# Where the second products of an expert and of a feed-forward stand in a stream that gives way to attention

## The chip, the cores and the metric

The kernel runs on one core of one Trainium2 chip. TensorE (PE in the profile) does the matrix products, with its weight loads (PEld) shown apart; VectorE (DVE), ScalarE (ACT) and GpSimd (POOL) do the element-wise work, and SyncE (SP) issues most transfers. Each engine works through its own instructions in a fixed order, which is settled when the program is built, and waits on semaphores for the others. The metric is the device time of one execution in microseconds: 1697.75 us is the median of three runs of the kernel before (1693.24 to 1705.93).

## The reference

The input is 2048 tokens of 128 float32 features. Two layers follow, each with a layernorm and a residual ahead of each half:

- layer 0, first half: a state-space mixer (8 heads, 16 states) with a gate;
- layer 0, second half: a block of its own, `x1 = x + attention(layernorm(x))`, and then `x1 + moe(layernorm(x1))`. The attention is causal, with 16 heads of 8 features over all 2048 tokens. The mixture has 8 experts of width 512, of which the two best of each token count; each expert is `gelu(n @ fc1.T + b1) @ fc2.T + b2`, scaled by the token's gate;
- layer 1, first half: a selective scan (256 channels, 16 states);
- layer 1, second half: a feed-forward, `h = silu(x w1) * (x w2)`, `h = gelu(h h1)`, `h = gelu(h h2)`, `h w3`, of width 512.

Everything is float32. All eight experts are computed for every token, and the gate of an expert that was not chosen is zero.

## The kernel before

**Chunks and stages.** The tokens are cut into four chunks of 512 (`NC`, `C`). Features lie on the 128 partitions, tokens along the free side, so most products are 128 by 128 times 128 by 512. The stages of a chunk are Python generators: `ssd`, `experts`, `scan`, `feed`, and for the attention `prepare`, `shift`, `weighted`, `conclude`. Each `yield` hands over with a number, the cost that the author gives to the piece just emitted.

**Attention beside the rest.** `with_attention` runs the generator of the stages, and after each piece of cost w it lets the attention go on until it has emitted pieces worth `w * RATE`. So a `yield` is a place where the stream of stages gives way, and its number says for how much attention. The attention goes job by job, a chunk of queries and a group of four heads: `shift` finds the maximum of the scores (products L304 into `ps_m`, mask L313, maximum on DVE L314), and `weighted` recomputes scores transposed (L354 into `ps_e`), adds the shift (L360), masks the diagonal (L362), takes the exponential on ACT (L364) and sums values (L341 into `ps_o`). `weighted` of one job and `shift` of the next are emitted in step. Each of `ps_m` and `ps_e` is one buffer of two banks, so a pair of score products waits until DVE, or ACT, has read the pair before. One pair of L354, its L360 pair and its exponential are called a step of attention here.

**An expert.** `experts` goes through the eight experts in pairs. For each pair it emits eight first products (L797, into the two buffers of `ps_a`), each followed by a gelu on ACT (L798). Then it yields 7.4, and the second products follow (L803): four of them sum into the single buffer of `ps_c`, one for each quarter of the hidden features, with a yield of 0.9 after each but the last. DVE adds the bias and multiplies by the gate (L807), POOL adds to the sum of the experts (L809), and a yield of 0.8 follows.

**Gelu and exponential take turns.** ACT has to load another table (a record of its own in the trace) between a gelu and an exponential. `in_turn` puts an order between the two kinds, so that the eight gelus of a pair stand together on ACT, and an exponential of the attention that is emitted after them waits behind them.

**A feed-forward.** `feed` has two inner layers (L954): for each of four output quarters f, four products k sum into a buffer of `ps_a`, with a yield of 0.9 after each but the last and 0.8 after the quarter. The gelus (L960) of two quarters are emitted together, behind every odd quarter. The third layer (L966) follows.

**What settles the order.** The emitted order gives priorities alone. A scheduler places the instructions on each engine, by its own estimate of when each is ready, so an instruction that is emitted later can stand earlier where the one ahead of it would wait. The result is the order of the built program.

**The tail.** The last chunk has no attention left beside it. It is cut into two halves of 256 tokens, and `abreast` alternates between `experts`, `scan` and `feed` of the halves and the `feed` of chunk 2, always taking the thread that is furthest behind by the sum of its yields. There the numbers of the yields decide how finely the threads alternate.

Of the kernel before, what the change touches and what calls it, by code (L numbers as in the profile page):

```python
# [24 lines left out]
NB = C // P  # L25
# [17 lines left out]
NF = FF // P  # L43
# [29 lines left out]
def two_layers(ctx: ExitStack, tc: tile.TileContext, a: dict, out: bass.AP):  # L73
# [27 lines left out]
    def col(name, i=0, n=P, w=1):  # L101
        at = COL[name][0] + i
        return cols[:n, at : at + w]
# [143 lines left out]
    def after_stage(*names):  # L247
        while not written.issuperset(names):
            yield None
# [471 lines left out]
    def part(c):  # L721

        c, lo, n = c if isinstance(c, tuple) else (c, 0, NB)
        return c, slice(lo, lo + n), n, n * P
# [3 lines left out]
    def turn(kind):  # L728
        used[kind] = used.get(kind, 1) ^ 1
        return used[kind]  # L730
# [6 lines left out]
    def experts(c, z):  # L737
        c, bs, NB, C = part(c)
        yield from after_stage(("attention", c))
        x = xc[c][:, bs]  # L740
        nx = z.blocks("xn", NB)
        layernorm(nx, xa[c][:, bs])
        pt = transposed(nx, z.bank)
        nT = z.line("nT", (P, C))
        nc.vector.tensor_scalar(nT, pt, col("ln2_w"), col("ln2_b"), ALU.mult, ALU.add)
        yield 1.0 * NB / 4

        pl = z.bank([P, NB, NE])
        for b in range(NB):
            nc.tensor.matmul(pl[:, b, :], nT[:, b * P : (b + 1) * P], w_eg, start=True, stop=True)  # L750
        lg = small_tile("lg", [P, NB, NE])
        nc.vector.tensor_copy(lg, pl)

        full = [P, NB, NE, NE]
        other = lg.unsqueeze(2).to_broadcast(full)
        own = lg.unsqueeze(3).to_broadcast(full)
        gt = small_tile("gt", full)
        eq = small_tile("eq", full)
        nc.vector.tensor_tensor(gt, other, own, ALU.is_gt)
        nc.vector.tensor_tensor(eq, other, own, ALU.is_equal)  # L760
        nc.vector.tensor_tensor(eq, eq, before8.unsqueeze(1).to_broadcast(full), ALU.mult)
        nc.vector.tensor_tensor(gt, gt, eq, ALU.add)
        rank = small_tile("rank", [P, NB, NE])
        nc.vector.tensor_reduce(rank, gt, AX.X, ALU.add)
        top = small_tile("etop", [P, NB])
        nc.vector.tensor_reduce(top, lg, AX.X, ALU.max)
        ge = small_tile("ge", [P, NB, NE])
        nc.vector.tensor_tensor(ge, lg, top.unsqueeze(2).to_broadcast([P, NB, NE]), ALU.subtract)
        nc.scalar.activation(ge, ge, AF.Exp)
        nc.vector.scalar_tensor_tensor(ge, rank, 1.5, ge, ALU.is_lt, ALU.mult)  # L770
        nc.vector.tensor_reduce(top, ge, AX.X, ALU.add)
        nc.vector.reciprocal(top, top)
        nc.vector.tensor_tensor(ge, ge, top.unsqueeze(2).to_broadcast([P, NB, NE]), ALU.mult)
        pgt = z.bank([NE, C])
        for b in range(NB):
            nc.tensor.transpose(pgt[:, b * P : (b + 1) * P], ge[:, b], ident)
        gT = z.line("gT", (NE, C))
        nc.vector.tensor_copy(gT, pgt)
        gates = scratch_g[turn("gates")][:, 0:C]
        nc.sync.dma_start(gates, gT)  # L780
        yield 1.5 * NB / 4

        acc = z.line("acc", (P, C))

        for e0 in range(0, NE, 2):
            of = []
            for e in (e0, e0 + 1):
                we = z.wide()
                nc.sync.dma_start(we[:, 0], a["fc1"][e])
                nc.sync.dma_start(we[:, 1].rearrange("p (k d) -> p k d", k=NF), a["fc2"][e].rearrange("(k p) d -> p k d", p=P))  # L790
                gb = z.line("gb", (P, C))
                nc.sync.dma_start(gb, gates[e].partition_broadcast(P))
                hs = [z.four("h", C) for _ in range(2)]
                of.append((we, gb, hs))
                for f in range(NF):
                    ph = z.bank([P, C])
                    nc.tensor.matmul(ph, we[:, 0, f * P : (f + 1) * P], nT, start=True, stop=True)  # L797
                    in_turn("gelu", nc.scalar.activation(hs[f // 2][:, f % 2, :], ph, AF.Gelu, bias=col("fc1_b", e * NF + f)))  # L798
            yield 7.4 * NB / 4
            for e, (we, gb, hs) in zip((e0, e0 + 1), of):  # L800
                py = z.sum([P, C])
                for f in range(NF):
                    nc.tensor.matmul(py, we[:, 1, f * P : (f + 1) * P], hs[f // 2][:, f % 2, :], start=f == 0, stop=f == NF - 1)  # L803
                    if f < NF - 1:
                        yield 0.9 * NB / 4
                dst = acc if e == 0 else z.line("ye", (P, C))
                nc.vector.scalar_tensor_tensor(dst, py, col("fc2_b", e), gb, ALU.add, ALU.mult)  # L807
                if e:
                    nc.gpsimd.tensor_tensor(acc, acc, dst, ALU.add)  # L809
                yield 0.8 * NB / 4  # L810
        pt = z.bank([P, NB, D])
        for b in range(NB):
            nc.tensor.transpose(pt[:, b, :], acc[:, b * P : (b + 1) * P], ident)
        nc.vector.tensor_tensor(x, x, pt, ALU.add)
        yield 1.0 * NB / 4
# [102 lines left out]
    def feed(c, z):  # L918
        c, bs, NB, C = part(c)
        x = xc[c][:, bs]  # L920
        nx = z.blocks("xn", NB)
        layernorm(nx, x)
        pt = transposed(nx, z.bank)
        nT = z.line("nT", (P, C))
        nc.vector.tensor_copy(nT, pt)
        w12 = z.wide()
        nc.sync.dma_start(w12[:, 0], a["w1"])
        nc.sync.dma_start(w12[:, 1], a["w2"])
        w3 = z.pool.tile([P, NF, D], F32, tag="w3", name="w3", bufs=1) if z.width < FF else z.blocks("w3")
        nc.sync.dma_start(w3, a["w3"].rearrange("(k p) o -> p k o", p=P))  # L930
        h = [z.four("h", C) for _ in range(2)]
        for f in range(NF):
            p1 = z.bank([P, C])
            nc.tensor.matmul(p1, w12[:, 0, f * P : (f + 1) * P], nT, start=True, stop=True)
            p2 = z.bank([P, C])
            nc.tensor.matmul(p2, w12[:, 1, f * P : (f + 1) * P], nT, start=True, stop=True)
            s = z.line("s", (P, C))
            in_turn("exp", nc.scalar.activation(s, p1, AF.Tanh, scale=half_s[:, f : f + 1]))
            nc.vector.scalar_tensor_tensor(s, s, 1.0, p1, ALU.add, ALU.mult)
            nc.vector.scalar_tensor_tensor(h[f // 2][:, f % 2, :], p2, both_s[:, f : f + 1], s, ALU.mult, ALU.mult)  # L940
            if f % 2:
                yield 3.5 * NB / 4
        for name, scale in (("h1", "h1_s"), ("h2", "h2_s")):
            w = []
            for i in range(2):
                w.append(z.wide())
                nc.sync.dma_start(w[i], a[name][2 * i * P : 2 * (i + 1) * P].rearrange("(k p) o -> p k o", p=P))
            g = [z.four("g", C) for _ in range(2)]
            phs = []
            for f in range(NF):  # L950
                ph = z.bank([P, C])
                phs.append(ph)
                for k in range(NF):
                    nc.tensor.matmul(  # L954
                        ph, w[k // 2][:, k % 2, f * P : (f + 1) * P], h[k // 2][:, k % 2, :], start=k == 0, stop=k == NF - 1
                    )
                    if k < NF - 1:
                        yield 0.9 * NB / 4
                for i in range(f - 1, f + 1) if f % 2 else ():
                    in_turn("gelu", nc.scalar.activation(g[i // 2][:, i % 2, :], phs[i], AF.Gelu, scale=col(scale, i)))  # L960
                yield 0.8 * NB / 4
            h = g
        po = z.sum([P, NB, D])
        for b in range(NB):
            for k in range(NF):
                nc.tensor.matmul(  # L966
                    po[:, b, :], h[k // 2][:, k % 2, b * P : (b + 1) * P], w3[:, k, :], start=k == 0, stop=k == NF - 1
                )
        res = z.blocks("xn", NB)
        nc.vector.tensor_tensor(res, po, row("w3_s").unsqueeze(1).to_broadcast([P, NB, D]), ALU.mult)  # L970
        nc.gpsimd.tensor_tensor(res, res, x, ALU.add)  # L971
        nc.sync.dma_start(x_out[c][:, bs], res)
        yield 3.6 * NB / 4
# [162 lines left out]
```

## Time and profile before

| what | value |
| --- | --- |
| median of three runs | 1697.75 us |
| the profiled execution, its own time | 1707.93 us |
| its span in the profile | 1706.2 us |
| PE busy | 1488.6 us, 87% |
| DVE busy | 983.1 us, 58% |
| ACT busy | 670.4 us, 39% |
| POOL busy | 265.1 us, 16% |
| mean granted TensorE clock | 0.847 |
| table loads on ACT, each | 1.283 us |

The profiled execution is 10.2 us longer than the median. The span is divided in time as follows: up to about 430 us the first layer's mixer, with the first attention jobs beside it from 160 us on; from 450 us to about 1450 us experts, scans and feed-forwards of chunks 0 to 2 with the attention; from there the tail. The twelve batches of eight gelus with attention beside them lie between 451 and 1209 us, four for each of the chunks 0, 1 and 2. A row of the view by windows gives, for a stretch of time, the busy time of PE, PEld, DVE, ACT and POOL with the number of their instructions, then the granted clock, the busy share of the DMA engines and GB/s. In the view of instructions in order of time, a row gives the start, the length, the engine, the line, the operation, and in brackets the idle time of the engine before it. A float32 product of 128 by 128 times 128 by 512 shows as two PE records.

### The profile page before, as it was taken

What the parts mean: (1) busy time and instruction counts of PE and PEld (TensorE: products, weight loads), DVE (VectorE), ACT (ScalarE), POOL (GpSimd) and SP (SyncE); (2) the same over time, 40 slices, a digit from 0 to 9 for tenths busy, and PEclk for the clock granted to TensorE, in tenths of its full rate; (3) what the DMA queues carried; (4) which work ended last, traced back from release to release, by engine and by line L of the source; (5) the groups of instructions that cost most, each with busy time, mean ns of one, the idle gap of its engine ahead of it and who ended that gap; (6) DMA issues with size and microseconds to landing.
All of it is one profiled execution on the core that took longest, in us unless ns stands there. A gap on an engine that the chain in (4) does not pass through costs nothing. (4 is left out here: it accounts for less than half of the span.)

```text
span 1706.2 us, 17298 instructions
## 1 busy us (share of the span) xinstructions
PE 1488.6 (87%) x6550; PEld 679.7 (40%) x6550; DVE 983.1 (58%) x1670; ACT 670.4 (39%) x864; POOL 265.1 (16%) x332
## 2 busy tenths in 40 slices
PE   6998999999999889887979868999888796889787
PEld 3554445454332333232333333433322232555355
DVE  4566546666444464658486878443568741337672
ACT  2212222332434334534425525445436463346351
POOL 3332011211000010122020122000001121112100
PEclk9898878898999787968779878887988876799798
DMA  2000000000211001246121535120103731334131
GB/s 87 1 1 1 1 0 1 1 1 1 79 38 37 25 25 33 76 103 142 35 52 32 123 74 112 38 62 29 40 24 68 151 80 32 114 100 129 40 91 52
DMA packets 73874, 90.93 MB, mean 53 GB/s; under 512 B 5672, under 2 KB 40696, under 8 KB 73792
## 3 DMA queue, kind: packets, MB, share of 16 engines
q1 hardware_dynamic: 61120, 65.18, 12.7%
q0 software_dynamic: 12240, 23.60, 8.2%
q8 instruction: 51, 0.84, 0.2%
q10 hardware_dynamic: 432, 1.06, 0.2%
q14 instruction: 31, 0.25, 0.1%
HBM read 64.98 MB, written 1.25 MB: 39 GB/s over the span
## 5 line engine op out<-in xcount | busy, mean ns | idle before, releaser
L314 DVE TENSOR_REDUCE top<-ps_m 128x2 f32<-128x1024 f32 (+3 forms) x320 | 339.5, 1061 | 267.9 <-PE ps_m L313 130.4
L364 ACT ACTIVATE probs<-ps_e 128x1024 f32<-128x1024 f32 (+3 forms) x320 | 286.6, 895 | 495.1 <-PE ps_e L360 268.0
L304 PE MATMUL ps_m<-kR,qR 32*128 32x512 f32 (+3 forms) x640 | 181.5, 519 | 57.7 <-DVE top L314 49.4
L354 PE MATMUL ps_e<-qR,kR 32*128 32x512 f32 (+3 forms) x640 | 174.0, 519 | 41.4 <-ACT probs L364 40.7
L884 DVE TENSOR_TENSOR_SCAN db<-da,hlast,db 128x512 f32<-128x512 f32 (+1 forms) x160 | 166.2, 1081 | 44.9 <-ACT da L880 44.2
L341 PE MATMUL ps_o<-probs,vv 128*9 128x512 f32 (+3 forms) x1152 | 175.0, 602 | 0.9 <-ACT probs L364 0.9
L304 PEld LDWEIGHTS ps_m<-kR,qR 32*128 32x128 f32 x640 | 74.1, 205 | 219.0 <-DVE top L314 127.1
L354 PEld LDWEIGHTS ps_e<-qR,kR 32*128 32x128 f32 x640 | 69.1, 204 | 200.5 <-ACT probs L364 132.6
L803 PE MATMUL ps_c<-h,wide 128*128 128x512 f32 (+1 forms) x320 | 142.5, 556 | 4.3 <-DVE ye L807 4.2
L360 PE MATMUL ps_e<-sh,onesR 32*128 32x512 f32 (+3 forms) x640 | 145.3, 430 | 1.1 <-DVE sh L326 1.1
L797 PE MATMUL ps_a<-nT,wide 128*128 128x512 f32 x192 | 107.5, 691 | 1.7 <-ACT h L798 1.6
L809 POOL TENSOR_TENSOR acc<-acc,ye 128x512 f32<-128x512 f32 (+1 forms) x35 | 41.1, 1174 | 395.8 <-DVE ye L807 360.4
L888 POOL COPY hlast<-db 128x2 f32<-128x2 f32 x64 | 26.7, 417 | 463.9 <-DVE db L884 456.5
L882 DVE TENSOR_TENSOR db<-du,bb 128x1024 f32<-128x1024 f32 (+1 forms) x80 | 79.9, 1016 | 20.2 <-DMA bb<-scratch_b 7.3
L798 ACT ACTIVATE h<-ps_a,cols 128x512 f32<-128x512 f32 x96 | 64.9, 687 | 54.4 <-PE ps_a L797 54.3
L880 ACT ACTIVATE da<-dl 128x1024 f32<-128x1024 f32 (+1 forms) x80 | 67.3, 880 | 29.7 <-DVE db L884 18.9
L803 PEld LDWEIGHTS ps_c<-h,wide 128*128 128x128 f32 x320 | 57.0, 198 | 52.4 <-issue 38.1
L360 PEld LDWEIGHTS ps_e<-sh,onesR 32*128 32x128 f32 x640 | 74.8, 219 | 6.2 <-issue 4.1
L954 PE MATMUL ps_a<-g,wide 128*128 128x512 f32 x96 | 60.4, 745 | 2.7 <-DVE sz L905 1.8
L797 PEld LDWEIGHTS ps_a<-nT,wide 128*128 128x128 f32 x192 | 35.6, 214 | 58.1 <-ACT h L798 39.7
L954 PE MATMUL ps_a<-h,wide 128*128 128x512 f32 x96 | 55.1, 678 | 0.0
L891 PE MATMUL ps_o<-db,ident 128*128 128x512 f32 x64 | 35.7, 640 | 7.7 <-DVE db L884 7.6
(376 smaller groups left out, 2072.2 us busy)
## 6 DMA issues: line engine op xcount, KB each, us to landing
wide<-in_fc SPq DMA_DIRECT2D x80, 256.0 KB, 3.2
bb<-scratch_b SPq DMA_DIRECT2D x48, 256.0 KB, 3.3
db<-db POOLq DMA_DIRECT2D x24, 512.0 KB, 5.5
u<-db POOLq DMA_DIRECT2D x21, 512.0 KB, 5.6
wide<-in_h SPq DMA_DIRECT2D x20, 512.0 KB, 3.9
gb<-scratch_g SPq DMA_DIRECT2D x24, 256.0 KB, 4.1
bb<-scratch_b SPq DMA_DIRECT2D x32, 128.0 KB, 3.0
wide<-in_w SPq DMA_DIRECT2D x10, 256.0 KB, 2.8
```

Source lines behind the costliest of these rows:

```text
L304: nc.tensor.matmul(pss[:, j, 0:n], qR[hr, w - P : w], kR[hr, g, kc * C : kc * C + n], start=True, stop=not diag,)
L314: nc.vector.tensor_reduce(top[:, i : i + 2, kc], pss[:, :, 0:n], AX.X, ALU.max)
L341: pv = nc.tensor.matmul(o, v, prs[i // 2][:, i % 2, q0:], start=kb == 0, stop=kb == nk - 1)
L354: nc.tensor.matmul(pss[:, j, q0:], kR[hr, g, kb * P : (kb + 1) * P], qR[hr, q0:], start=True, stop=False)
L360: nc.tensor.matmul(pss[:, j, q0:], onesR[hr], sh[hr, q0:], start=False, stop=not diag)
L364: last = nc.scalar.activation(pr[:, :, q0:], pss[:, :, q0:], AF.Exp, scale=float(1.0 / np.sqrt(np.float32(HD))))
L797: nc.tensor.matmul(ph, we[:, 0, f * P : (f + 1) * P], nT, start=True, stop=True)
L803: nc.tensor.matmul(py, we[:, 1, f * P : (f + 1) * P], hs[f // 2][:, f % 2, :], start=f == 0, stop=f == NF - 1)
L880: in_turn("exp", nc.scalar.activation(das[i], dl, AF.Exp, scale=-float(i + 1)))
L882: nc.vector.tensor_tensor(db, du, bb.unsqueeze(1).to_broadcast(two), ALU.mult)
L884: nc.vector.tensor_tensor_scan(db[:, j, :], das[n][:, j, :], db[:, j, :], hlast[:, j, n : n + 1], ALU.mult, ALU.add)
L954: nc.tensor.matmul(ph, w[k // 2][:, k % 2, f * P : (f + 1) * P], h[k // 2][:, k % 2, :], start=k == 0, stop=k == NF - 1)
```

## The change

In `experts` the yield of 7.4 behind the batch of gelus goes, and the four second products of the first expert of the pair are emitted directly behind the batch, with no yield between them. Then comes one yield of 10.1, which is 7.4 and three times 0.9, and after it the first expert's L807. The second expert keeps its yields. In `feed`, the yield of 0.8 behind the first pair of gelus goes, the first two products of quarter 2 are emitted directly behind these gelus, and a yield of 2.6 follows them, which is 0.8 and twice 0.9. The sum of the yields of a stage is as before, and so is every instruction; positions alone change. The lines of the changed kernel behind this place stand 2, and behind `feed` 6, lower down (L807 becomes L809, L954 becomes L956, L960 becomes L965).

```diff
                     in_turn("gelu", nc.scalar.activation(hs[f // 2][:, f % 2, :], ph, AF.Gelu, bias=col("fc1_b", e * NF + f)))
-            yield 7.4 * NB / 4
+
             for e, (we, gb, hs) in zip((e0, e0 + 1), of):
                 py = z.sum([P, C])
                 for f in range(NF):
                     nc.tensor.matmul(py, we[:, 1, f * P : (f + 1) * P], hs[f // 2][:, f % 2, :], start=f == 0, stop=f == NF - 1)
-                    if f < NF - 1:
+                    if f < NF - 1 and e > e0:
                         yield 0.9 * NB / 4
+                if e == e0:
+                    yield 10.1 * NB / 4
                 dst = acc if e == 0 else z.line("ye", (P, C))
                 nc.vector.scalar_tensor_tensor(dst, py, col("fc2_b", e), gb, ALU.add, ALU.mult)
...
-                    if k < NF - 1:
+
+                    if k == 1 and f % 2 == 0 and f:
+                        yield 2.6 * NB / 4
+                    elif k < NF - 1 and (k or f % 2 or not f):
                         yield 0.9 * NB / 4
                 for i in range(f - 1, f + 1) if f % 2 else ():
                     in_turn("gelu", nc.scalar.activation(g[i // 2][:, i % 2, :], phs[i], AF.Gelu, scale=col(scale, i)))
-                yield 0.8 * NB / 4
+                if f % 2 == 0 or f == NF - 1:
+                    yield 0.8 * NB / 4
```

## The prediction

> **What bounds the kernel now.** I read the page's busy shares first: PE is busy for 87% of the span, no other engine over 58%, so time is won on PE's idle time or on its clock alone. The change aims at one place, the time behind a batch of eight gelus, when the exponentials still wait for the gelus and the table. So the second view is the busy time by windows, over the 4 us behind the end of each of the twelve batches (end of the last gelu in the view in order of time; five of twelve rows and the sum are shown). The columns after the length are PE, PEld, DVE, ACT and POOL, then the granted clock.
>
> ```profile
> 460.40:464.40 4.00, 4.00 (x13) 1.71 (x13) 0.27 (x2) 3.18 (x4) 0.00 (x0) 1.00 0.00 0
> 499.50:503.50 4.00, 4.00 (x18) 1.80 (x16) 1.76 (x4) 1.90 (x3) 0.00 (x0) 1.00 0.00 0
> 543.60:547.60 4.00, 4.00 (x16) 1.46 (x14) 2.27 (x3) 2.30 (x2) 0.00 (x0) 1.00 0.00 0
> ...
> 768.10:772.10 4.00, 3.75 (x12) 1.20 (x10) 3.62 (x4) 3.99 (x4) 0.00 (x0) 1.00 0.20 63
> 837.20:841.20 4.00, 4.00 (x15) 1.41 (x14) 2.29 (x3) 3.99 (x4) 0.00 (x0) 1.00 0.00 0
> ...
> sum 48.00, PE 47.76 PEld 16.85 DVE 22.89 ACT 34.35 POOL 0.00; mean PE 3.98 PEld 1.40 DVE 1.91 ACT 2.86 POOL 0.00
> ```
>
> PE is busy for 47.76 of 48 us there, at full clock. The hole is already filled: in the order of the built program, 31 second products (four for each of the twelve batches would be 48) stand between the last L797 of a batch and the next L354, and with them 15 pairs of L304. The third view is the same windows for the stretches between batches; three of ten are shown.
>
> ```profile
> 463.30:489.10 25.80, 24.42 (x113) 9.56 (x112) 12.00 (x17) 7.93 (x10) 1.27 (x1) 0.97 0.21 62
> 714.60:756.20 41.60, 34.29 (x162) 11.88 (x160) 30.52 (x29) 14.45 (x18) 11.45 (x12) 0.68 0.60 133
> 771.60:823.30 51.70, 41.49 (x146) 12.98 (x145) 36.14 (x37) 19.28 (x21) 11.70 (x14) 0.76 0.52 114
> ```
>
> Here the time goes: over the ten stretches PE is busy for 305 of 347.5 us, and the clock, weighted by length, is 0.83; if it is either whole or half, that is half clock for 34% of the time. The last view, PE's waits from 430 to 1450 us, says on what.
>
> ```profile
> PE ps_m L304 <- DVE top L314: 43.3, 48, 2.4
> PE ps_e L354 <- ACT probs L364: 40.3, 49, 1.8
> ...
> PE ps_c L803 <- DVE ye L807: 3.1, 3, 1.7
> ```
>
> Two single buffers, one read by DVE's maximum and one by the exponential, end most of PE's idle time. Both belong to the steps of attention.
>
> **What a step costs.** In the view in order of time:
>
> ```profile
> 511.31 0.50 PE L354 MATMUL ps_e<-qR,kR 32*128 32x512 f32 x2
> 511.31 0.50 PE L304 MATMUL ps_m<-kR,qR 32*128 32x512 f32 x2
> ...
> 511.64 0.40 PE L360 MATMUL ps_e<-sh,onesR 32*128 32x512 f32 x2
> ...
> 512.14 1.02 ACT L364 ACTIVATE probs<-ps_e 128x1024 f32<-128x1024 f32 x1 [1.51 <-PE ps_e L360]
> ...
> 513.40 0.50 PE L304 MATMUL ps_m<-kR,qR 32*128 32x512 f32 x2 [0.31 <-DVE top L314]
> ```
>
> The next L354 starts at 513.41: a step takes 2.10 us, a circle of products, exponential and two hand-overs. PE works 0.33 us on L354 (a pair of L304 beside it starts in the same instant and is free), 0.33 on L360 and half of a round of L341 (eight records, 1.02 us from 547.61 to the next product), 0.51: 1.17 in all. A second product is two records at 0.43 to 0.53 us, so 0.96. At full clock a step with one product needs 2.13 us of PE, against the 2.10 it takes anyway; at half clock it needs 4.26, where a step without one needs 2.34.
>
> **The change, part by part.**
>
> 1. *Behind the batches.* In the changed order all twelve batches have exactly four second products behind them, 48 in place of 31, and 3 pairs of L304 in place of 15. PE idles for 0.24 us in these windows now, so filling them better gives at most 0.2: **0**. Nor is it a loss: from the last first product to the next L354 passed 3.8 us in the third batch (542.8 to 546.6), and four products are 3.8.
> 2. *17 products leave the steps.* One frees 0.03 us at full clock and 1.9 at half: 17 × 0.34 × 1.9 = 11 us if the clock stays as it is. But half clock comes where steps are thin, and they get thinner: in the changed order 89 of 192 full-sized steps hold no other product, before 82. If the half-clock time were not touched by the moved products, the gain is 17 × 0.03, 0.5 us. With nothing to choose by, I take the middle: **-5.5**.
> 3. *12 pairs of L304 come into the steps.* PE has them free beside L354. DVE's maximum is 1.22 us, and its own circle was 1.83 us (513.40 to 515.23), just under a step, so the cost is 0 where DVE does nothing else. Where a scan runs beside (the rows from 714.6 and 771.6: DVE busy for 73% and 70%) each takes DVE time that is wanted: 5 of the 15 pairs stood behind batches five to eight, 1 does now, so 4 × 0.72 × 1.22 = **+3.5**. Upper end 12 × 1.83 = 22, lower end 0.
> 4. *L807 of the first expert* is emitted 10.1 later and has more time until the second expert's products need `ps_c` again. The waits of L803 for L807 are 3.1 us; I take **-2**, bounds -3.1 and 0. POOL's L809 behind it has waited 360 us in all for L807 and delays only the end of a stage.
> 5. *The feed-forwards.* Beside the attention there are four places where quarter 2 follows a pair of gelus. In the changed order two, four, three and four steps of attention stand ahead of its first product, the same numbers as before. The reason is in the emitted work: quarter 2 needs a buffer of `ps_a`, and both are held until the gelus have read them, so the scheduler takes what is ready. **0**, bounds -2 and +2, one product of 0.96 hidden or exposed in two of the four.
> 6. *The tail* has coarser yields, and this shows on ACT: the changed order has 82 table loads, before 77, and all five more stand in the tail, where exponentials of a scan now come between the gelus of the second half's experts (the profile's 1530 to 1590). A load is 1.283 us, so 6.4 us more of ACT, with its queue of gelus behind each load, and PE's L797 behind these, since they need the banks. ACT is busy for 25.37 of 40 us from 1510 to 1550; I count the loads at that share, 0.63 × 6.4 = **+4**, bounds 0 (PE, 89% busy, hides them) and 6.4.
> 7. *Transfers.* An expert's weights are free earlier by the move, and SP's loads of the next ones with them. PE's waits of over 0.3 us from 430 to 1450 name no weight transfer as their end: **0** both ways.
>
> Sum: 0 - 5.5 + 3.5 - 2 + 0 + 4 + 0 = 0. A profiled execution stays at 1707.9; the median of the runs shown is 10.2 below that, so **1698 us**. The bounds add up to -16.3 (11, 0.2, 2 and 3.1) and +29.9 (22, 2 and 6.4, less 0.5), but hardly all at once.
>
> A rule speaks against the change. The Trainium skill, "TensorE: Matmul & The Clock Gate", Part 1, says that the clock halves after an idle activity window of about 3.4 us and needs a busy one to come back. The trace shows clocks of 1.00 behind the batches and of 0.68 in a thin stretch, though PE's single gaps are below 2.5 us with few exceptions; so idle time need not fill the window here. By the rule, as an estimate, each further run of three or more empty steps costs up to 1.7 us; there are 16 such runs in the changed order and 15 before, so the sum would be 2 us higher.
>
> **The rivals.**
>
> *Faster: the stretches are PE's.* For it: 88% busy, and half clock for a third of the time, in which a product costs its step 1.9 us. Then part 2 gives its 11 us, part 4 its 3, and L304 pairs that stood alone at 0.43 us (515.23 to 515.66) and now stand beside L354 give 12 × 0.43 = 5; the tail hides its loads. -19, or 1679 us. Against it: the two largest waits of PE are for the circles of attention.
>
> *Slower: DVE's maximum becomes the bound of the steps.* One mechanism in one place: behind a batch, where DVE was busy for 22.89 of 48 us, it has done a maximum or two ahead; now it stands still there and has 12 more to do in the steps. The point from which it decides: DVE's other work per step over 2.10 - 1.83 = 0.27 us. In the scan stretches it is over that; in the first chunk's stretch (12.00 of 25.80 busy) it is not. Price: 22 us if all 12 count at 1.83, less 5.5 for part 2 and 2 for part 4, with the tail's 6.4: +21, or 1719 us. For it: the wait for L314 is PE's longest.
>
> *It does not do what it says.* The scheduler had done most of it already, and in `feed` still does not do it. Then parts 2 to 4 shrink, and the tail's loads alone remain: 0 to +6, inside the forecast's own range.
>
> **How the numbers follow.** The forecast with the third rival, within 1% (1681 to 1715), has 0.46; the faster rival 0.22; the slower one 0.32, more than its opposite since the tail's five loads are certain and the hole was not there. About 1% is what a measurement of this kernel can tell from no change: the three runs shown differ by 0.7%. The range takes in both rivals with a few us of the bounds beyond, 1675 to 1724; outside are the ends where nearly all bounds add up.
>
> **What would show it.** If right: the 4 us behind the batches stay at full PE and clock; DVE's busy time there falls from 22.89 by some 12 to 15; the waits of L304 for L314 grow and those of L354 for L364 shrink by similar sums; ACT has 82 table loads; the tail is some 4 us longer. The prediction is wrong downwards if the clock of the stretches rises above 0.83, and upwards if the wait for L314 grows by over 15 us, or if the tail's loads hold up DVE's scan too.

## The result, and the profile after

The changed kernel takes 1733.58 us (median of four runs, 1729.88 to 1748.07), the kernel before beside it 1695.49 (four runs, 1681.82 to 1705.93). The ratio is 1.0258, with a 95% interval of 1.0203 to 1.0314. It is formed of fast runs alone and is not the quotient of the two medians: between the medians the kernel is slower by 38 us, by the ratio by 44. Either way the time lies above the predicted range. The profiled execution of the changed kernel has a span of 1728.2 us and an own time of 1729.88. Before, the profiled one was 10 us above its median; now it is 4 below, so the two profiles differ by 22 us where the medians differ by 38. The clocks differ in the same way: 0.847 and 0.845 in the two profiles, but 0.833 to 0.845 in the four runs of the changed kernel, and medians of 0.852 to 0.856 for the kernel before in the later comparisons.

The windows of 4 us behind the twelve batches of gelus of the changed kernel, four rows and the sum (columns as before):

```profile
458.88:462.88 4.00, 4.00 (x14) 1.62 (x13) 1.12 (x2) 2.88 (x4) 0.00 (x0) 1.00 0.10 7
544.70:548.70 4.00, 4.00 (x16) 1.62 (x15) 1.25 (x2) 2.50 (x4) 0.35 (x1) 1.00 0.10 11
...
775.80:779.80 4.00, 4.00 (x14) 2.08 (x13) 1.60 (x2) 3.29 (x3) 0.00 (x0) 1.00 0.06 18
841.95:845.95 4.00, 4.00 (x16) 1.38 (x16) 1.01 (x2) 3.97 (x5) 0.00 (x0) 1.00 0.09 14
...
sum 48.00, PE 48.00 PEld 18.03 DVE 12.62 ACT 33.70 POOL 2.15; mean PE 4.00 PEld 1.50 DVE 1.05 ACT 2.81 POOL 0.18
```

The change did what it was written to do. PE has no gap there any more, and DVE, with fewer maxima to do, works 12.62 us in place of 22.89. To see where the loss is, the same view cuts the span at the last exponential of the attention: first row the attended part (from the first batch of gelus on), second row the tail. Before:

```profile
451.80:1449.20 997.40, 866.96 (x3735) 327.17 (x3734) 587.07 (x768) 445.03 (x505) 130.37 (x143) 0.82 0.27 62
1449.20:1706.20 257.00, 213.37 (x748) 135.32 (x748) 132.10 (x286) 102.42 (x175) 35.08 (x52) 0.88 0.30 87
```

After:

```profile
450.30:1477.70 1027.40, 863.54 (x3735) 327.09 (x3734) 584.63 (x768) 444.72 (x505) 131.10 (x143) 0.82 0.26 60
1477.70:1728.20 250.50, 207.55 (x748) 133.29 (x748) 131.83 (x286) 108.63 (x179) 36.25 (x52) 0.90 0.31 90
```

The attended part is 30.0 us longer with the same number of PE records, the same clock in these two profiles and 3.4 us less of PE's work: PE idles for 163.9 us (length less busy time) where it idled for 130.4. The tail is 6.5 us *shorter*, though ACT has 6.2 us more to do in it; PE's idle time there is as before (43.6 and 43.0), the clock is higher (0.88 and 0.90).

What ends the idle time of the attended part, PE's waits from 430 to 1480 us of the changed kernel (total, times, longest):

```profile
PE ps_m L304 <- DVE top L314: 63.2, 56, 6.3
PE ps_e L354 <- ACT probs L364: 45.1, 49, 4.0
PE ps_c L915 <- POOL u L911: 9.3, 2, 4.6
...
PE ps_c L803 <- DVE ye L809: 2.2, 2, 1.1
```

The wait for the maximum grew from 43.3 to 63.2 us, but only from 48 to 56 times, and its longest from 2.4 to 6.3: not every step is a little later, a few are very late. What was late on DVE then? Two rows of each page point at the answer: the instruction `db = du * bb` in the scan, by which DVE fills a new scan buffer, and a transfer of 512 KB that adds such a buffer to a sum. Before:

```profile
L882 DVE TENSOR_TENSOR db<-du,bb 128x1024 f32<-128x1024 f32 (+1 forms) x80 | 79.9, 1016 | 20.2 <-DMA bb<-scratch_b 7.3
...
u<-db POOLq DMA_DIRECT2D x21, 512.0 KB, 5.6
```

After:

```profile
L884 DVE TENSOR_TENSOR db<-du,bb 128x1024 f32<-128x1024 f32 (+1 forms) x80 | 81.4, 1034 | 26.8 <-issue 17.7
...
u<-db POOLq DMA_DIRECT2D x21, 512.0 KB, 6.1
```

DVE stands still for 17.7 us ahead of this instruction (7.0 before), with no engine as the cause ("issue"). In the list of DVE's waits from 640 to 1480 us (total, times, longest) these are, before and after:

```profile
DVE db L882 <- issue: 7.0, 3, 3.6
```

```profile
DVE db L884 <- issue: 17.7, 5, 5.6
```

The scan's code says for what. It is not among the functions that the change touches:

```python
scans = Stream("s", wk, 8, 4, ("a",), "c")        # 8 buffers of the size that z.four gives
...
            db = z.four("db", C)
            nc.vector.tensor_tensor(db, du, bb..., ALU.mult)
...
                nc.gpsimd.dma_start(sums[n % 2], db, accum_op=ALU.add)
```

A state's `db` is added to one of two sums by a transfer of 512 KB, and its buffer is free when this transfer has landed. In the changed kernel, in order of time:

```profile
734.58 1.20 DVE L884 TENSOR_TENSOR db<-du,bb 128x1024 f32<-128x1024 f32 x1
...
735.77 1.19 POOL L897 DMA_DIRECT2D db<-db  x1
735.81 0.32 SPq L879 DMA_DIRECT2D bb<-scratch_b  x1
736.22 0.38 SPq L789 DMA_DIRECT2D wide<-in_fc  x1
736.65 0.43 SPq L790 DMA_DIRECT2D wide<-in_fc  x1
736.83 2.45 DVE L886 TENSOR_TENSOR_SCAN db<-da,hlast,db 128x512 f32<-128x512 f32 x2
...
739.59 1.19 POOL L897 DMA_DIRECT2D u<-db  x1
743.95 1.23 DVE L884 TENSOR_TENSOR db<-du,bb 128x1024 f32<-128x1024 f32 x1 [4.66 <-issue]
745.09 0.95 DVE L314 TENSOR_REDUCE top<-ps_m 128x2 f32<-128x768 f32 x1
...
746.10 0.69 PE L304 MATMUL ps_m<-kR,qR 32*128 32x384 f32 x2 [6.26 <-DVE top L314]
```

Two loads of weights start right behind the accumulating transfer of 735.77, which lands at 743.87, after 8.1 us (the pages' medians for such transfers are 5.4 to 6.1). DVE's next L884 starts 0.08 us later. (The profile names no releaser; but the same 0.08 us lies between a landing at 1338.76 and the start at 1338.84, and in the two parts of the change, run alone below, between 746.31 and 746.39 and between 1320.07 and 1320.15.) The attention's maximum L314 had its scores, mask included, since 738.1, but it stands behind L884 on DVE; so PE waits 6.26 us with L304, and ACT's next exponential waits 8.15. It happens again at 1338.84, where L884 has waited 5.58 us, for a transfer that took 9.0 us beside a load for `feed`, and PE waited 5.23. In the kernel before, a transfer issued at 737.36, with the same loads around it, took 8.5 us too, and nothing waited; the product that waits in the changed kernel, the sixth of this scan, had started at 736.17, ahead of it:

```profile
738.16 2.45 DVE L884 TENSOR_TENSOR_SCAN db<-da,hlast,db 128x512 f32<-128x512 f32 x2
740.53 0.72 DVE L807 SCALAR_TENSOR_TENSOR ye<-ps_c,cols,gb 128x512 f32<-128x512 f32 x1
741.17 0.95 DVE L314 TENSOR_REDUCE top<-ps_m 128x2 f32<-128x768 f32 x1
742.15 0.17 DVE L316 TENSOR_REDUCE low<-top 128x4 f32<-128x12 f32 x1
743.00 1.23 DVE L314 TENSOR_REDUCE top<-ps_m 128x2 f32<-128x1024 f32 x1 [0.69 <-PE ps_m L304]
```

(Its L884 is the scan; its L882, the product, comes next at 760.67 in DVE's order.) So at this place it is not the slow transfer that is new, but what stands behind it in DVE's order. Nor are such waits new: the longest of the three before, 3.56 us, ends at 731.53, again 0.08 us behind the landing of a transfer, which took 8.6 us with no load of weights begun near it.

A second place is the end of a job of attention, in a stretch without a scan. After:

```profile
563.29 1.98 PE L797 MATMUL ps_a<-nT,wide 128*128 128x512 f32 x4
565.21 0.50 PE L304 MATMUL ps_m<-kR,qR 32*128 32x512 f32 x2
567.04 0.50 PE L304 MATMUL ps_m<-kR,qR 32*128 32x512 f32 x2 [1.33 <-DVE top L314]
567.47 0.28 PE L313 MATMUL ps_m<-mask_qk,ident 128*128 128x128 bf16 x2
569.07 0.50 PE L304 MATMUL ps_m<-kR,qR 32*128 32x512 f32 x2 [1.32 <-DVE top L314]
```

The job's exponentials are through, but two more pairs of scores of `shift` are still owed, and there is nothing else in PE's order. Before, the same pairs stand between second products (a pair of L304 at 558.36, 560.61 and 563.03, an L803 or L797 behind each), and PE has one gap of 0.41. From the last exponential of this job to the first of the next, 11.5 us pass before and 16.7 after.

So there were three candidates: scan buffers, maxima that are owed at the end of a job, and, as the third line of PE's waits shows, the products at the end of a scan (L915, behind POOL's L911), for which PE waited twice, 9.3 us in all; before, once, for 4.8.

### The profile page after: what moved, and what is told of

It is laid out like the page before. It is cut to its first block, busy times and chain, and to the rows that moved or that the text cites. A ratio compares the mean times of both kernels' runs of the same rounds, so it can differ in the third digit from the quotient of the medians.

```text
span 1728.2 us, 17295 instructions
## 1 busy us (share of the span) xinstructions
PE 1479.4 (86%) x6550; PEld 679.6 (39%) x6550; DVE 980.1 (57%) x1670; ACT 676.0 (39%) x869; POOL 266.8 (15%) x332
## 4 chain that ended last, share of the span: by engine, by line
PE 61%; DVE 18%; issue 8%; ACT 6%; DMA 5%; POOL 2%; SPq 0%; ACTq 0%; POOLq 0%; DVEq 0%
PE ps_o L341 8%; PE ps_a L797 5%; DVE top L314 5%; PE ps_c L803 5%; PE ps_m L304 5%; PE ps_e L354 5%; DVE db L886 4%; PE ps_e L360 3%; ACT probs L364 3%; PE ps_a L956 2%; PE ps_c L593 2%; DMA u<-db 2%; PE ps_a L551 2%; PE ps_a L568 2%; DMA db<-db 2%
## 5 line engine op out<-in xcount | busy, mean ns | idle before, releaser
L364 ACT ACTIVATE probs<-ps_e 128x1024 f32<-128x1024 f32 (+3 forms) x320 | 286.2, 894 | 504.3 <-PE ps_e L360 291.3
L314 DVE TENSOR_REDUCE top<-ps_m 128x2 f32<-128x1024 f32 (+3 forms) x320 | 339.4, 1061 | 200.3 <-PE ps_m L304 100.6
L304 PE MATMUL ps_m<-kR,qR 32*128 32x512 f32 (+3 forms) x640 | 178.8, 520 | 83.4 <-DVE top L314 68.8
L354 PE MATMUL ps_e<-qR,kR 32*128 32x512 f32 (+3 forms) x640 | 171.7, 517 | 47.3 <-ACT probs L364 45.5
L341 PE MATMUL ps_o<-probs,vv 128*9 128x512 f32 (+3 forms) x1152 | 183.0, 610 | 1.5 <-ACT probs L364 1.3
L304 PEld LDWEIGHTS ps_m<-kR,qR 32*128 32x128 f32 x640 | 73.2, 205 | 229.3 <-DVE top L314 148.5
L354 PEld LDWEIGHTS ps_e<-qR,kR 32*128 32x128 f32 x640 | 68.5, 204 | 208.0 <-ACT probs L364 141.3
L803 PE MATMUL ps_c<-h,wide 128*128 128x512 f32 (+1 forms) x320 | 130.7, 528 | 2.9 <-DVE ye L809 2.2
L797 PE MATMUL ps_a<-nT,wide 128*128 128x512 f32 x192 | 108.3, 696 | 2.2 <-ACT h L798 2.2
L884 DVE TENSOR_TENSOR db<-du,bb 128x1024 f32<-128x1024 f32 (+1 forms) x80 | 81.4, 1034 | 26.8 <-issue 17.7
L882 ACT ACTIVATE da<-dl 128x1024 f32<-128x1024 f32 (+1 forms) x80 | 67.3, 879 | 41.1 <-DVE db L886 23.8
L803 PEld LDWEIGHTS ps_c<-h,wide 128*128 128x128 f32 x320 | 58.2, 193 | 50.8 <-issue 40.6
L809 DVE SCALAR_TENSOR_TENSOR ye<-ps_c,cols,gb 128x512 f32<-128x512 f32 (+1 forms) x35 | 22.4, 640 | 85.4 <-PE ps_c L803 81.4
L797 PEld LDWEIGHTS ps_a<-nT,wide 128*128 128x128 f32 x192 | 35.2, 215 | 56.2 <-ACT h L798 40.4
L956 PE MATMUL ps_a<-g,wide 128*128 128x512 f32 x96 | 55.6, 691 | 0.8 <-DVE x L916 0.5
L956 PE MATMUL ps_a<-h,wide 128*128 128x512 f32 x96 | 55.6, 687 | 0.0
```

The lines of the kernel that those rows point to most:

```text
L304: nc.tensor.matmul(pss[:, j, 0:n], qR[hr, w - P : w], kR[hr, g, kc * C : kc * C + n], start=True, stop=not diag,)
L314: nc.vector.tensor_reduce(top[:, i : i + 2, kc], pss[:, :, 0:n], AX.X, ALU.max)
L341: pv = nc.tensor.matmul(o, v, prs[i // 2][:, i % 2, q0:], start=kb == 0, stop=kb == nk - 1)
L354: nc.tensor.matmul(pss[:, j, q0:], kR[hr, g, kb * P : (kb + 1) * P], qR[hr, q0:], start=True, stop=False)
L364: last = nc.scalar.activation(pr[:, :, q0:], pss[:, :, q0:], AF.Exp, scale=float(1.0 / np.sqrt(np.float32(HD))))
L882: in_turn("exp", nc.scalar.activation(das[i], dl, AF.Exp, scale=-float(i + 1)))
```

## The experiments

**Which part.** The two parts of the change can be taken alone: `experts` changed and `feed` as before, and the reverse. (The cut is written as in the same pair with nine buffers, further down; here the one function is simply as before, which comes to the same.)

```diff
+            behind = True               # in experts; in feed: behind = False, and the reverse
+            if not behind:
+                yield 7.4 * NB / 4
...
-                if e == e0:
+                if e == e0 and behind:
                     yield 10.1 * NB / 4
```

> The change in experts alone, feed as before. Theory A (the loss sits in the two stages in which a feed-forward runs beside a scan, and is made by the new yields of feed: the traces of before and after differ there by 11 and 15 us of the 28 that the part with attention lost): within 0.7% of before, a ratio of 0.995 to 1.007. Theory B (the experts' second products are missed in the steps of attention): the whole loss, 1.020 to 1.030. Theory C (any move redraws the whole order, and the time scatters): anything from 0.99 to 1.03, with no tie to the place of the edit.

> The change in feed alone, experts as before. Theory A: most of the loss, a ratio of 1.015 to 1.028, with the first stage of the experts (to about 640 us) as before to a microsecond or two. Theory B: 0.995 to 1.005. Theory C: anything from 0.99 to 1.03, and also a different time in the tail, whose order the feed's yields touch.

The expert part gives 1724.94 us, 1.0149 (1.0085 to 1.0213); the feed-forward part 1714.77, 1.0109 (1.0060 to 1.0157). They add up to 2.58%, the whole, though each is known to 0.5 or 0.6% only, and both kernels lie outside what theories A and B said of them. The long wait of the first scan is in the one (L884 starts at 746.39 after 4.77 us, PE waits 6.37) and the second one's in the other (5.37 us at 1320.15, PE waits 6.62). This decides nothing yet between the causes, but the feed-forward part moves no maximum behind a batch of expert gelus, and has two fifths of the loss.

**Smaller yields.** 7.4 became 7.3 in `experts` and one 0.8 became 0.85, meant as a new order with no purpose.

```diff
-            yield 7.4 * NB / 4
+            yield 7.3 * NB / 4
...
-                yield 0.8 * NB / 4
+                yield 0.85 * NB / 4
```

> The kernel before with two numbers a little changed (7.4 to 7.3, and 0.8 behind an expert to 0.85, so that the sum over a pair of experts stays): no product is moved by hand. Theories A and B: within 0.5% of before. Theory C: the order is redrawn and the time differs from before by 1% or more, either way.

The order on PE came out as before's, so that this is the same program again: 1698.05 us, 0.9981 (0.9938 to 1.0024). So it does not say whether any new order costs time (theory C). It gives a scale, though: its profiled execution was 16 us ahead of before's at about 1180 us, with the same instructions in the same order. In its attended part PE is busy for 850.8 us and idle for 134.0 at a clock of 0.84, in before's 867.0 and 130.4 at 0.82. So of two executions of one order the busy time differs with the clock by 16 us, and the idle time by 4.

**A ninth scan buffer.**

```diff
-    scans = Stream("s", wk, 8, 4, ("a",), "c")
+    scans = Stream("s", wk, 9, 4, ("a",), "c")
```

With the whole change, and as a control in the kernel before:

> The changed kernel, with a ninth buffer for the scan's large tiles (eight before). Theory D (in the stretches with a scan, part of the loss is DVE standing still ahead of the scan's product db<-du,bb until an accumulating transfer has freed a buffer, with the attention's maximum queued behind it: 4.8 us of idle DVE at 742 us with the change in experts alone, 5.4 us at 1315 us with the change in feed alone): these two long waits of L304 for L314, 6.26 and 5.23 us in the changed kernel, are gone, and the time falls by 10 to 18 us against the changed kernel, a ratio to before of 1.012 to 1.019. Theory C (it is the order as such): no tie between the buffer and these waits, and the ratio stays near 1.025 or goes anywhere.

> The kernel before with the same ninth buffer, as a control. Theory D: it has no such wait of over 5 us, so it gains little, a ratio of 0.993 to 1.001. If it gains as much as the changed kernel does, the buffer is a gain of its own and says nothing on the change.

The changed kernel comes down from 1.0258 to 1.0059 (1.0029 to 1.0089; 1702.26 us), more than the expected 1.012 to 1.019; the kernel before stays, 0.9993 (0.9961 to 1.0025). By the ratios the buffer takes away some 34 us of 44, and it is worth nothing without the change. PE's waits of the changed kernel with nine buffers, 430 to 1450 us:

```profile
PE ps_m L304 <- DVE top L314: 48.3, 53, 2.5
PE ps_e L354 <- ACT probs L364: 46.7, 46, 3.7
```

The long waits for the maximum are gone (longest 2.5 us), and DVE's product never waits for "issue" again. The rival that the maxima themselves had become the bound falls here: behind the batches of this kernel DVE is busy for 12.64 us, so as many maxima stand in the steps as in the changed kernel, and most of the loss is gone. The ninth buffer is not a pure removal of a wait: the scheduler places the instructions anew from the first scan on, and the weight loads of 736 us stand elsewhere too. In the profiles the attended part falls from 1027.4 to 993.2 us. Of these 34.2 us 16.4 are idle time of PE (147.5 us are left), about as much as the waits for the maximum lost; the other 17.8 are shorter work of PE at a clock of 0.84 in place of 0.82, which two executions of one order can differ by as well.

The same with each part alone:

> The expert part of the change alone, with a ninth scan buffer. It cost 1.49% with eight. Theory: the wait for the buffer near 742 us, with the stretch of halved clock behind it, goes, and the end of the job near 567 us stays: 0.4 to 0.7% are left, 1.004 to 1.007. Rival: the ninth buffer helps only the feed-forward part, and 1.49% stays, 1.012 or above.

> The feed-forward part of the change alone, with a ninth scan buffer. It cost 1.09% with eight. Theory: the wait for the buffer near 1315 us was most of it, and 0 to 0.4% is left, 1.000 to 1.004. Rival: the cost is in the feed-forward's own products behind the gelus, for which a scan buffer does nothing: 1.008 or above.

The expert part falls from 1.0149 to 1.0024 (0.9997 to 1.0051), the feed-forward part from 1.0109 to 1.0006 (0.9978 to 1.0035). With the buffer both losses are gone or nearly so (the tail's part in these ratios comes next). For the expert part this is better than expected, though its end of a job at 570 us is as long as in the changed kernel (16.7 us).

**The tail alone.** The change only where no attention stands beside it, with eight buffers and with nine.

```diff
+            behind = c == NC - 1        # in feed: behind = c >= 2; else all as before
```

> The change in the last part alone, which has no attention (the experts and the feed-forwards of the last chunk's halves, and the feed-forward of chunk 2); elsewhere the order of before. The traces show 257 us for that part before and 250.5 us with the change, in spite of five more table loads. If that is the order's doing, the tail takes 249 to 252 us and the ratio is 0.995 to 0.998; if the gain came from what stands ahead of it or from the clock, 255 to 258 us and 0.998 to 1.003. My forecast counted 4 us of loss here: 1.002.

> The change only where no attention stands beside it (experts of chunk 3, feed-forward of chunks 2 and 3), with a ninth scan buffer. With eight buffers this was 0.9971. Theory: in the stages beside the attention nothing is moved, so a ninth buffer does nothing, and the tail gains 3 to 7 us as before: 0.995 to 0.999. Rival: the tail's scans also want the ninth buffer, and 10 us or more come off: below 0.994.

The ratios are 0.9971 (0.9933 to 1.0009; 1693.86 us) and 0.9948 (0.9916 to 0.9979; 1688.90 us). In the profiled executions the tails are 249.4 and 249.9 us long, before 257.0 (256.6 in the kernel with smaller yields, 256.8 in the kernel before with nine buffers). So the tail gains, five more table loads and all, though the first of the two ratios alone does not show it; and the second of these kernels is faster than both the kernel before and the changed one. It also corrects the account: against 0.9948 the attended part of the change with nine buffers still costs 1.1% (1.0059 / 0.9948), some 19 us.

**The end of the job.** As the change, but the pair of experts 4 and 5 of chunk 0 as before; first with eight buffers in a single run, then with nine.

```diff
+            behind = (c, e0) != (0, 4)  # in feed: behind = True
```

> The changed kernel, but the third pair of experts of the first chunk is emitted as before (yield of 7.4 behind its gelus). Theory E (behind a batch the maximum of the attention is now not fed, and the maxima that are owed stand alone at the end of the job of attention, 1.83 to 2.03 us each with PE idle for 1.3 of them): the three waits of 1.3 us for L314 around 567 to 571 us are gone, and from the 92nd to the 96th exponential of the attention it takes 17 us as before, not 23 as with the change; what follows is as in the changed kernel, so that the whole is 4 to 8 us shorter than it. If the 6 us come from elsewhere, they stay.

> The whole change, but the pair of experts 4 and 5 of chunk 0 is emitted as before, and the scan's stream has nine buffers of the kind of db and u, not eight. If the loss is made of the waits on DVE for a scan buffer (taken away by the ninth buffer, which left 1.0059) and of the maxima left over at the end of a job (17 us there before, 11 with this pair as before, so 6 us or 0.4%), the ratio falls to 1.002, and the interval holds 1.0. Rival: what was left at 1.0059 is spread over all steps, by maxima that are late everywhere. Then this pair is one of twelve and the ratio stays at 1.005 or above.

In both the place itself is as before (11.5 and 11.7 us between the exponentials, from 16.7). The single run gave 1730.45 us, at a mean clock of 0.840, and shows no gain in the whole; with nine buffers it is 1.0026 (0.9991 to 1.0061), from 1.0059. That is the expected size, but the two intervals overlap: the local 5.2 us are shown, their worth in the whole is not.

**The end of the scan.** Also the pair 6 and 7 of chunk 1 as before, with nine buffers. This brings the products of the scan's end back behind one more product of an expert.

```diff
-            behind = (c, e0) != (0, 4)
+            behind = (c, e0) not in ((0, 4), (1, 6))
```

> As the version with nine scan buffers and the pair of experts 4 and 5 of chunk 0 as before, and now also the pair 6 and 7 of chunk 1 as before: the products of the scan's end (w_out, behind the POOL product with sz) then stand in PE's order where they stand before the change, behind one more product of an expert. In every kernel with the expert edit, with eight buffers or nine, PE waits 4.4 to 4.7 us there at the end of chunk 0's scan; without the edit 0.6 us. Theory: that wait is the next 4 us of what was left: it falls from 4.63 to below 1 us, and the ratio from 1.0026 to 0.999 to 1.001. Rival: PE's wait there is covered by what the attention owes elsewhere: the wait goes, but the ratio stays at 1.002 to 1.005. In the comparison with the change in the tail alone (0.9948), 0.8% was left unexplained; the theory takes away a third of it.

PE's waits for POOL at the ends of the first and the third scan, without this step and with it, each from its kernel's list of waits:

```profile
PE ps_c L917 <- POOL u L913: 9.3, 2, 4.7
```

```profile
PE ps_c L917 <- POOL u L913: 2.4, 2, 1.8
```

The wait of 4.63 us at 866, which the step is about, is down to 0.58. (The other, at about 1420, fell from 4.70 to 1.79, but two executions of the order before have 4.82 and 2.66 there.) And between the 164th and the 172nd exponential, the stretch around it, this kernel gains 5.0 us on the one without the step. The whole is 1692.31 us, 0.9975 (0.9942 to 1.0008). Ten of the twelve pairs and all of `feed` are as in the change, and no loss is left that can be measured: against the tail's gain alone, 0.3% (0.9975 / 0.9948). By these ratios the change cost the attended part some 53 us (1.0258 / 0.9948, of 1697; 49 against the tail alone with eight buffers, 0.9971): 34 for the scan buffers, 6 for the end of the job, 9 for the end of the scan, 5 left over. All but the first are near their own uncertainty of some 8 us or below it.

PE's idle time in the attended part, from the profiles, goes the same way with smaller sums: 163.9 us in the changed kernel, 147.5 with the ninth buffer, 145.9 with the end of the job as before too, 136.5 with the end of the scan as well, and 130.2 to 136.1 in five kernels in which nothing is moved there. The idle time that the change added is accounted for by place, then. The rest of the loss shows as a lower clock, and why it is lower was not separated.

## Why the prediction was wrong

- *What bounds the kernel* held: most of PE's idle time is the attention's circles, and the hole behind the batches was not there. Part 1 (0) came as said, 48.00 of 48 us, and DVE's busy time fell there by 10.3 (12 to 15 said). Of the other signs, the waits of L354 for L364 did not shrink: they grew from 40.3 to 45.1 us.
- *Part 2* (-5.5) and *part 4* (-2) could not be seen by themselves; the wait of part 4 fell from 3.1 to 2.2 us. The doubt in part 2, that thinner steps lose clock, is not settled: the two profiles have 0.82 both, but the kernel before has 0.84 in its second execution, and the runs of the changed kernel have lower clocks than most of its runs. If all of that is the change's doing, it costs about 13 us (an estimate: PE's 863.5 us less the 850.8 of the second execution). The Trainium skill, "TensorE: Matmul & The Clock Gate", Part 1, with its idle window, was set against the change there with an estimate of 2 us. At one place the trace agrees: in the changed kernel the clock goes to half at 741.6 us, within PE's gap of 6.26 us, and stays there for 30.7 us. But in the kernel before it goes to half at 740.1 us for 23.9 us, and from 725 to 745 us PE has no gap over 1.3 us.
- *Part 3* (+3.5) counted the maxima that come into the steps and charged DVE's own time for them. With nine buffers as many of them stand in the steps, and the expert part costs 0.24%, 4 us, the tail's gain included. The size is in the stated bounds, but the place was not seen: the one place where such maxima were found to cost time, 5.2 us at 570 us, is the end of a job with nothing beside it, not the scan's stretches.
- *Part 5* (0, with 2 us each way) failed too. It looked for the products behind the gelus and found their places unchanged, which was true; but the feed-forward part cost 1.09%, 18 us, and a scan buffer takes that away (1.0006). The code has a step that the prediction did not take: it counted the coarser yields for `abreast` in the tail alone, but `second_layers` lets the three scans go `abreast` of `experts(1)`, `feed(0)` and `feed(1)` in the same way. With the feed-forward part alone DVE's order is before's up to about 950 us, where the first of these feed-forwards stands beside a scan, and differs from there on. That the coarser yields move the scan's pieces was not tested apart.
- *Part 7* (0 both ways) is **the step that failed most**. It asked of transfers only whether PE waits for a weight load, and PE does not, before or after. It left out the scan's own transfers: they hold the buffers that DVE's product needs, and DVE's order has the attention's maximum behind that product. So the sum has no term for a wait that took 17.7 us of DVE's time, 7.0 before, with PE idle for 6.26 and 5.23 us behind the two longest of it; a ninth buffer takes away some 34 of the 44 us by the ratios, and 16.4 of the 33.5 us of added idle time. The list of PE's waits before names only the last link, "L304 <- DVE top L314", but the 7.0 us of "issue" ahead of L882 were there to be seen: three waits, a sign that eight buffers were only just enough.
- *Part 6* (+4) had the five loads right (82) and the sign wrong: the tail gained 6.5 us in the profile, and 0.3 to 0.5% alone. PE's idle time in the tail did not grow by them, and its granted clock rose from 0.88 to 0.90. The clock is not the reason: the kernel before with nine buffers has 0.90 there too and takes 256.8 us. Why the new alternation gains was not tested.
- *The rivals.* The slower one had the sign and half the size (1719), and its announced sign came: the wait for L314 grew by 19.9 us, over the 15 that the prediction named. Its mechanism was wrong all the same: 14.9 of these 19.9 go with a ninth buffer, which takes no maximum out of the steps. A total that moves as a rival says is no proof of the rival; its count and its longest wait were the better witnesses. The faster rival fell with the time, and its sign did not come: the clock did not rise in the attended part (0.82 both); and that the change does not do what it says fell with the windows behind the batches.

What stays open: whether the transfer is slow because of the loads beside it (in the changed kernel the 21 accumulating transfers between 600 and 1480 us with a load of weights begun in the 5 us before their issue or until they land took 6.9 us in the median, the other 24 took 5.2; before, 5.9 and 5.2, but up to 8.6 without such a load), since no run separated the loads from the order; how much of the ninth buffer's effect is its new order; and how much of the loss is the lower clock of the changed kernel's runs, and what lowers it.

## What to carry to other kernels

Where an engine works through a fixed order, a wait ahead of one stage's instruction is a wait for every other stage behind it: before something is moved, look for the instructions of *other* stages that wait for a buffer on the engine that feeds the critical circle, and ask which transfer frees it, what the move puts beside this transfer, and whether it puts the waiting instruction behind it. In a list of waits, read the count and the longest beside the total. And where a change loses, test its parts by place: here the last seventh of the program gained from the same edit that cost the part before it about 3%.

## What was not expected of the hardware

A transfer of 512 KB that accumulates took 5.2 us in the median with no weight load near it and up to 9.1 us with one in the changed kernel; in the kernel before one without a load took 8.6. The same program, run twice, was 16 us apart at about 1180 us of its span, at mean granted clocks of 0.847 and 0.855. And five more table loads, 1.283 us each on ACT, stand in a tail that is 6.5 us shorter.
